# Column counts of a four-layer graph kernel: partial counts on the vector engine in place of count matmuls

## The chip, the cores and the metric

The kernel runs on one core of one Trainium2 (trn2) chip. The metric is the device time of one execution in microseconds (us). Each kernel was timed in rounds that alternate it with the kernel before on the same chip.

The engines in the profile are PE (TensorE, matmuls), PEld (its weight loads), DVE (VectorE), ACT (ScalarE), POOL (GpSimd) and SP. L552 means line 552 of that kernel's source; the lines after the edit move by 18, so L541 of the kernel before and L559 of the kernel after are both the count matmul.

## The reference, cut to what matters

Four graph layers work on `x` (2708 x 512) with one dense 2708 x 2708 adjacency matrix. Only the first layer is touched:

```python
def _L0_gnn_ref(cur, incidence_m):
    mask = incidence_m > 0
    head = mask.astype(incidence_m.dtype)
    head = head / jnp.maximum(jnp.sqrt(jnp.sum(head * head, axis=-1, keepdims=True)), EPS)
    inc = incidence_m + head
    edge_fea = inc @ cur
    edge_degree = jnp.sum(inc, axis=-1, keepdims=True)
    return edge_fea / edge_degree
...
x = _layernorm(x + _L0_gnn_ref(x, adj), axis=-1)
```

So before the product can start for some nodes, the number of nonzero entries of their rows of `adj` must be known: `inc` is `adj` plus `count ** -0.5` wherever `adj` is nonzero.

## The kernel before

The kernel holds `adj` transposed, so a destination node is a column and a count runs down the partitions. One pass over the matrix is a *sweep*; the first sweep is layer 0. It goes through four *ranges* of destination columns (256, 384, 384 and 330 wide, numbered 0 to 3), each in two halves h = 0 and 1 of the matrix, and each half has 22 row tiles of 128 rows. Ranges 1 to 3 use a seven-product scheme for 2 x 2 blocks, which needs sums of blocks such as s1 = A21 + A22, made by the vector engine just ahead of the matmuls that use them. While range r is multiplied, the counts of range r + 1 are made:

```python
def count_load(R0, n, h, i):            # GpSimd queue: one row tile of the later range
    ...
def count_mask(R0, n, h, i, t=None, on_vector=False):
    ...
    cnt[R0, h, i] = m = mask_tile()     # bf16, 128 x 384, six buffers
    ...
        nc.scalar.activation(m[:w, :n], t[:w, :n], AF.Sign)
        nc.scalar.activation(m[:w, :n], m[:w, :n], AF.Relu)

def count_tile(R0, n, h, i):            # TensorE: three matmuls of one column
    w = wt(i % KT)
    m = cnt.pop((R0, h, i))
    if i == 0:
        cnt[h] = bank("cnt", [P, 4])
    for j, q in enumerate(tiles_of(R0, n)):
        wq = wt(q)
        nc.tensor.matmul(cnt[h][:wq, j : j + 1], m[:w, q * P - R0 : q * P - R0 + wq], ones_bf[:w, 0:1],
                         start=i == 0 and j == 0, stop=i == NT - 1, skip_group_check=True)

def count_row(R0, n, h):                # clamp on VectorE, power on GpSimd
    ...
        nc.vector.tensor_scalar(r[: wt(q), 0, j : j + 1], ps[: wt(q), j : j + 1], 1.0, None, ALU.max)
    nc.gpsimd.tensor_tensor(r[:, 1, :m], r[:, 0, :m], neg_half.to_broadcast([P, m]), ALU.pow)

def spread_row(R0, n, h):               # TensorE transposes it into a row, ScalarE copies it
    ...
        nc.tensor.transpose(pr[:, q * P - R0 : q * P - R0 + w], r[:w, 1, j : j + 1].to_broadcast([w, P]), ident[:w, :w])
    nc.scalar.copy(row[R0, h][:, :n], pr[:, :n])

def prep0(r, R0, n, h, hj, k, a):       # VectorE: adj + mask * count ** -0.5
    nc.vector.scalar_tensor_tensor(t[:w, :n], a[:w, :n], 0.0, row[R0, h][:w, :n], ALU.is_gt, ALU.mult)
    nc.vector.tensor_tensor(a[:w, :n], a[:w, :n], t[:w, :n], ALU.add)
```

The schedule is a list of events `at(position, function)`; a unit is one phase (one product) of a range. For the later range's half h:

```python
for i in range(NT):                     # NT = 22
    q = pb + p + d * i / NT
    at(q - 0.7, lambda i=i, h=h: count_load(R1, n1, h, i))
    at(q - 0.35, lambda i=i, h=h: count_mask(R1, n1, h, i))
    at(q, lambda i=i, h=h: count_tile(R1, n1, h, i))
at(pb + p + d, lambda h=h: count_row(R1, n1, h))
at(pb + p + d + 0.15, lambda h=h: spread_row(R1, n1, h))
```

TensorE takes its matmuls in the program's order (in this kernel's trace it waits 2.28 us for a mask in front of the count triple at 90.07 us, with large matmuls behind it).

## Time and profile before

| | kernel before |
|---|---|
| median of its first 3 runs | 2988.14 us (2979.09 to 2988.84) |
| profiled span, clock | 2983.9 us, 0.994 |
| VectorE busy, 62 to 460 us | 340 of 398 us |
| TensorE's waits that the profile names, 62 to 460 us | 7.3 us |
| second sweep's first matmul | 439.2 us |

The table is read so: the edit can act only in the first sweep, so the start of the second sweep says what the edit was worth there. TensorE hardly waits between 62 us and that point; the lines are shown in the prediction.

```profile
286.64 2.47 POOL L555 TENSOR_TENSOR r<-r,neg_half 128x3 f32<-128x3 f32 x1 [19.75 <-DVE r L553]
```

After the last count triple TensorE has 12 large matmul records before the transposes, about 4 us. The power ends at 286.64 + 2.47 = 289.11 us, and the transposes start at 289.98: hidden, with 0.9 us to spare.

### The profile page before, as it was taken

Reading aid. Unit: us, or ns where it says so; the run is one execution under the profiler, and the core shown is the slowest. Engines: PE = TensorE matmul, PEld = TensorE weight load, DVE = VectorE, ACT = ScalarE, POOL = GpSimd, SP = SyncE. Lnnn points to the kernel's source line nnn. Section 1 sums busy time; section 2 is a strip of 40 time slices with the busy share of each in tenths; the row PEclk is TensorE's granted clock in tenths of the full one; section 3 lists DMA queues with packets and bytes.
Section 4 is the critical chain, followed back from the end, with each engine's and each line's share of the span. In section 5 each row is a group of like instructions: output and inputs, shape, how many; then the busy total and the mean of one; then the engine's idle time right before and its main releaser. Section 6 shows DMA issues by size and latency. Waiting matters only on the chain.

```text
span 2983.9 us, 37755 instructions
## 1 busy us (share of the span) xinstructions
PE 2930.5 (98%) x10982; PEld 1926.6 (65%) x10982; DVE 2191.4 (73%) x5376; ACT 596.3 (20%) x1145; POOL 692.6 (23%) x1240
## 2 busy tenths in 40 slices
PE   7999999999999999999999999999999999999998
PEld 6655666557665657766666666666666666665664
DVE  5889688556657675874686777867768877689786
ACT  4544200000144444551101000010000100100001
POOL 1423224233410101213112022020220322512112
PEclk9999999999999999999999999999999999999999
DMA  7665467586754333654676667565675666875562
GB/s 233 199 198 176 143 179 217 141 136 138 192 113 124 110 112 94 202 158 143 199 218 212 183 194 219 169 208 178 196 225 174 196 200 197 242 199 179 172 177 83
DMA packets 364119, 524.27 MB, mean 176 GB/s; under 512 B 57734, under 2 KB 312430, under 8 KB 363912
## 3 DMA queue, kind: packets, MB, share of 16 engines
q1 hardware_dynamic: 297556, 362.80, 43.4%
q0 software_dynamic: 57040, 148.22, 16.1%
q10 hardware_dynamic: 9316, 10.84, 1.2%
q8 instruction: 87, 1.43, 0.2%
q14 instruction: 120, 0.98, 0.1%
HBM read 431.26 MB, written 90.37 MB: 175 GB/s over the span
## 4 chain that ended last, share of the span: by engine, by line
PE 84%; issue 5%; DVE 4%; DMA 4%; ACT 1%; POOL 1%; SPq 1%; POOLq 0%; DVEq 0%; ACTq 0%
PE accc L1007 12%; PE accd L1007 12%; PE accu L1007 12%; PE ps_d L495 9%; PE accu L367 8%; PE accc L367 8%; PE accd L367 7%; PE acca L1007 6%; PE acca L367 4%; PE ps_n L1076 1%; PE accc L1012 1%; PE accu L1012 1%; PE accd L1012 1%; PE acca L1012 1%; SPq L127 1%
## 5 line engine op out<-in xcount | busy, mean ns | idle before, releaser
L967 DVE TENSOR_TENSOR z<-z 128x339 f32<-128x339 f32 (+1 forms) x966 | 468.8, 507 | 35.6 <-PE accu L1007 12.5
L1007 PE MATMUL accc<-z,t 128*128 128x338 f32 (+1 forms) x644 | 203.0, 447 | 0.0
L1007 PE MATMUL accc<-s,t 128*128 128x338 f32 (+1 forms) x644 | 197.9, 452 | 1.0 <-DVE s L967 1.0
L1007 PE MATMUL accd<-z,t 128*128 128x338 f32 (+1 forms) x644 | 195.2, 448 | 0.0
L1007 PE MATMUL accu<-z,t 128*128 128x338 f32 (+1 forms) x644 | 194.9, 448 | 0.0
L331 DVE TENSOR_TENSOR a<-a,a 128x384 f32<-128x384 f32 (+4 forms) x363 | 177.4, 511 | 13.9 <-PE accu L367 13.4
L1039 DVE TENSOR_TENSOR q<-q,accd 128x338 f32<-128x338 f32 (+1 forms) x112 | 56.4, 504 | 173.2 <-PE accd L1007 170.8
L1033 ACT COPY q<-accu 128x338 f32<-128x338 f32 (+1 forms) x84 | 34.3, 443 | 721.2 <-PE accu L1007 721.2
L449 POOL TENSOR_TENSOR rstd<-rstd,neg_half 128x1 f32<-128x1 f32 (+3 forms) x92 | 61.5, 668 | 495.1 <-DVE rstd L448 494.2
L967 DVE TENSOR_TENSOR s<-z 128x338 f32<-128x338 f32 (+1 forms) x322 | 154.2, 505 | 23.4 <-PE accc L1007 20.6
L1007 PEld LDWEIGHTS accc<-z,t 128*128 128x128 f32 x644 | 121.4, 189 | 61.3 <-issue 2.2
L1007 PEld LDWEIGHTS accc<-s,t 128*128 128x128 f32 x644 | 121.6, 192 | 59.8 <-issue 2.5
L1007 PEld LDWEIGHTS accu<-z,t 128*128 128x128 f32 x644 | 121.0, 190 | 59.0 <-issue 1.5
L1007 PEld LDWEIGHTS accd<-z,t 128*128 128x128 f32 x644 | 120.8, 190 | 58.3 <-issue 1.9
L757 DVE SCALAR_TENSOR_TENSOR deg<-a,deg 128x384 f32<-128x384 f32 (+5 forms) x168 | 81.5, 504 | 68.1 <-DMA a<-in_adjT 67.8
L127 POOL DMA_DIRECT2D Y<-y x102 | 55.3, 543 | 280.3 <-ACT y L1089 192.8
L822 ACT ACTIVATE e<-row,neg_s 128x384 f32<-128x384 f32 (+5 forms) x176 | 100.5, 571 | 86.5 <-DVE e L824 23.9
L824 DVE TENSOR_TENSOR e<-e,f 128x384 f32<-128x384 f32 (+5 forms) x176 | 87.3, 504 | 25.3 <-ACT f L823 24.2
L823 ACT ACTIVATE f<-row,neg_s 128x384 f32<-128x384 f32 (+5 forms) x176 | 99.9, 567 | 12.6 <-PE accc L367 6.4
L127 POOL DMA_DIRECT2D As<-a x132 | 71.2, 543 | 107.1 <-DVE a L331 48.8
L1089 ACT COPY y<-ps_n 128x512 f32<-128x512 f32 (+2 forms) x48 | 28.0, 584 | 322.3 <-issue 175.6
L495 PE MATMUL ps_d<-w,q 128*128 128x512 f32 (+2 forms) x192 | 88.1, 604 | 3.5 <-DVE q L1145 3.4
(655 smaller groups left out, 6173.5 us busy)
## 6 DMA issues: line engine op xcount, KB each, us to landing
z<-As SPq DMA_DIRECT2D x320, 169.5 KB
z<-As SPq DMA_DIRECT2D x320, 169.0 KB
a<-in_adjT SPq DMA_DIRECT2D x240, 192.0 KB
z<-in_adjT SPq DMA_DIRECT2D x240, 169.5 KB
z<-in_adjT SPq DMA_DIRECT2D x240, 169.0 KB
a<-in_adjT SPq DMA_DIRECT2D x120, 165.0 KB
cl<-in_adjT POOLq DMA_DIRECT2D x80, 192.0 KB, 4.5
a<-in_adjT SPq DMA_DIRECT2D x113, 128.0 KB
```

Source lines behind the costliest of these rows:

```text
L127: queue.dma_start(out=dst[:c], in_=src[:c])
L331: nc.vector.tensor_tensor(A[r, dst, k][:w, :n], A[r, a, k][:w, :n], A[r, b, k][:w, :n], op)
L367: nc.tensor.matmul(B[home, c][:, :n], X[STAT[p], k][:w, c * P : (c + 1) * P], A[r, MOV[p], k][:w, :n], start=bool(start and k == k0), stop ...
L449: nc.gpsimd.tensor_tensor(rstd[:w, 1:2], rstd[:w, 0:1], neg_half[:w], ALU.pow)
L495: nc.tensor.matmul(o, lhs(c), r, start=c == 0 and n == 0, stop=c == DC - 1, skip_group_check=True)
L757: nc.vector.scalar_tensor_tensor(d[:w, :n], a[:w, :n], 0.0, d[:w, :n], ALU.not_equal, ALU.add)
L822: nc.scalar.activation(e[:w, :n], row[R0, h][0][:w, :n], AF.Exp, bias=neg_s[:w, t : t + 1])
L823: nc.scalar.activation(f[:w, :n], row[R0, h][1][:w, :n], AF.Exp, bias=neg_s01[:w, t : t + 1])
L824: nc.vector.tensor_tensor(e[:w, :n], e[:w, :n], f[:w, :n], ALU.min)
L967: nc.vector.tensor_tensor(d[:, :n], Z[x + (k,)][:, :n], Z[y + (k,)][:, :n], op)
L1007: nc.tensor.matmul(B[home][:, :n], stat(v, k), a[:, :n], start=bool(start and k == 0), stop=k == nk - 1, skip_group_check=True)
L1012: nc.tensor.matmul(B[home][:, :n], groups[st, "R"][0][:w, c * P : (c + 1) * P], Z[p, 2, 0][:w, :n], start=False, stop=True, skip_group_che ...
```

## The change

Its intent: TensorE looks full, and 22 x 3 one-column matmuls per half-range are poor use of it. The masks are 0 or 1 in bf16, so 22 of them can be summed elementwise without rounding on the vector engine, and one triple of matmuls then counts the half-range.

```diff
+    def count_add(R0, n, h, i):
+
+        w = wt(i % KT)
+        m = cnt.pop((R0, h, i))
+        if i == 0:
+            cnt[h] = pool.tile([P, 384], BF, name="ca", tag="tmp", bufs=NTMP)
+            nc.vector.tensor_copy(cnt[h][:w, :n], m[:w, :n])
+        else:
+            nc.vector.tensor_tensor(cnt[h][:w, :n], cnt[h][:w, :n], m[:w, :n], ALU.add)
+
+    def count_end(R0, n, h):
+        t = cnt[h]
+        cnt[h] = bank("cnt", [P, 4])
+        for j, q in enumerate(tiles_of(R0, n)):
+            wq = wt(q)
+            nc.tensor.matmul(cnt[h][:wq, j : j + 1], t[:, q * P - R0 : q * P - R0 + wq], ones_bf[:, 0:1], start=True,
+                             stop=True)
+
...
-                    at(q, lambda i=i, h=h: count_tile(R1, n1, h, i))
+                    at(q, lambda i=i, h=h: count_add(R1, n1, h, i))
+                at(pb + p + d - 0.02, lambda h=h: count_end(R1, n1, h))
                 at(pb + p + d, lambda h=h: count_row(R1, n1, h))
                 at(pb + p + d + 0.15, lambda h=h: spread_row(R1, n1, h))
```

## The prediction

> **What bounds the kernel now.** I first read the page: busy shares, and the busy digits by slice.
>
> ```profile
> PE 2930.5 (98%) x10982; PEld 1926.6 (65%) x10982; DVE 2191.4 (73%) x5376; ACT 596.3 (20%) x1145; POOL 692.6 (23%) x1240
> PE   7999999999999999999999999999999999999998
> DVE  5889688556657675874686777867768877689786
> ```
>
> TensorE (PE) looks like the bound of the whole kernel, with VectorE (DVE) at 73%. But the change touches only the first sweep (the first 5 to 6 slices of 75 us), and there the DVE digits are 8, 8, 9. So I asked for the busy time of the first sweep's four ranges; from the accumulators' names, the ranges begin near 20, 120, 231 and 342 us. The first of these stretches starts at 62 us, where the counts for later ranges begin.
>
> ```profile
> 62.00:120.00 58.00, 55.38 (x357) 45.18 (x356) 49.85 (x138) 40.84 (x90) 28.60 (x52) 0.97 0.65 202
> 120.00:231.00 111.00, 111.00 (x482) 65.69 (x481) 99.72 (x244) 55.61 (x115) 34.36 (x61) 1.00 0.68 211
> 231.00:342.00 111.00, 111.00 (x482) 66.12 (x481) 88.52 (x209) 43.72 (x90) 32.98 (x55) 1.00 0.50 150
> 342.00:439.00 97.00, 93.45 (x348) 63.80 (x347) 83.45 (x211) 5.04 (x9) 25.23 (x46) 0.96 0.58 170
> ```
>
> The columns are stretch, length, then busy us of PE, PEld, DVE, ACT, POOL. PE is full in ranges 1 and 2, but DVE has only 11 and 22 us of idle time there. The views of waits say how near DVE is to the path (waiter <- releaser: us, times, longest):
>
> ```profile
> PE rs L590 <- DVE run L573: 3.2, 1, 3.2
> PE accd L367 <- DVE a L331: 0.3, 1, 0.3
> DVE r L553 <- PE cnt L541: 14.7, 6, 10.4
> DVE rd L620 <- PE rs L590: 6.5, 3, 4.3
> DVE ld L635 <- PE ps_n L478: 5.8, 4, 3.3
> ```
>
> I also matched each PE wait on DVE in the trace with the moment DVE released it. The matmuls on the sum "s1" (accd with T1, third phase of a range) start 0.04 us after their release at 162.6 us (range 1), about 5.8 us after at 271 (range 2), and 0.05 us after at 375 (range 3). So PE is full, and DVE is exactly at its heels twice. There are two bounds, and the change moves work from one to the other.
>
> **What the skill says.** "VectorE: DVE Perf Modes", the perf-mode tier table: tensor_tensor runs at 1x in fp32 and at 2x in bf16 in SBUF. The trace has no bf16 two-source add; for fp32 it agrees: the pitch below grows by 0.13 us for 128 more elements, 1.04 ns each. "TensorE: Matmul & The Clock Gate", Back-to-back issue gap: a matmul of 1 to 64 columns takes about 60 cycles, 25 ns at the stated 2.4 GHz, when isolated, more with a weight load. Here it is about 53 ns with its load (below). "Perfetto Trace Analysis", Identifying the Most-Contended Engine: matmul busy time isn't a good measure, since matmuls are pipelined. The trace agrees: a count matmul is recorded as 163 ns and occupies a third of that.
>
> **The change, part by part.** It removes the 22 x 3 count matmuls of each of six half-ranges: 396, replaced by 18. Their price is in the chain of waits: start, us, what.
>
> ```profile
> 126.26 3.87 PE accu L367 x12
> ...
> 137.08 1.40 PE accc L367 x4
> 138.48 0.05 PE cnt L541 x3
> ```
>
> Twelve large matmuls alone take 3.87 us, 0.3225 each, so four take 1.29. With a count triple, the group repeats every 1.40 + 0.05 = 1.45 us. A triple costs 0.16 us, and 132 triples 21 us; the six final triples give back about 1. PE also waits in front of count matmuls for masks from ACT, about 3 us between 62 and 100 us. Were PE the only bound, the time would fall by 20 to 24 us, to about 2966.
>
> It adds 132 DVE instructions: 126 bf16 adds and 6 copies, 88 of 384 columns and 44 of 330. The price is the pitch on DVE, not the recorded duration, as instructions overlap:
>
> ```profile
> 101.73 0.55 DVE L578 SCALAR_TENSOR_TENSOR s<-a,row 128x384 f32<-128x384 f32 x1
> 102.20 0.42 DVE L203 TENSOR_TENSOR T2A<-B22A,T1A 128x256 f32<-128x256 f32 x1
> 102.54 0.42 DVE L205 TENSOR_TENSOR T3A<-B22A,T3A 128x256 f32<-128x256 f32 x1
> ```
>
> 384 columns have a pitch of 0.47 us, 256 of 0.34: 0.07 fixed plus 1/0.96 ns a column. At 2x, 384 bf16 columns are an estimate of 0.07 + 0.20 = 0.27 us (recorded about 0.35), 330 are 0.24. An add set between two dependent adds costs less, about 0.15, because the dependent pair now pays 0.455 for 256 columns against 0.335 undisturbed. In all 21 x 0.27 + 11 x 0.15 + 56 x 0.27 + 44 x 0.24 = 33 us more on DVE. ACT's masks and the loads are unchanged; mask buffers now come free when DVE, not PE, has read them.
>
> **Where this lands.** The order in which the built program puts the instructions on DVE has 32 of the adds ahead of the first T3 sum, 53 ahead of range 1's last s1, 97 ahead of range 2's, all 132 ahead of range 3's. The final count also needs the last add, so PE is tied to DVE at six points. In the kernel before, DVE's lead there was small:
>
> ```profile
> 220.73 0.29 DVE L553 TENSOR_SCALAR r<-cnt 128x1 f32<-128x1 f32 x3 [1.50 <-PE cnt L541]
> 286.20 0.29 DVE L553 TENSOR_SCALAR r<-cnt 128x1 f32<-128x1 f32 x3 [0.15 <-PE cnt L541]
> 332.27 0.29 DVE L553 TENSOR_SCALAR r<-cnt 128x1 f32<-128x1 f32 x3 [1.46 <-PE cnt L541]
> ```
>
> The ledger of DVE's lateness D, adds minus the waits on PE (all in the trace) that a late DVE no longer has: at 99.5 us, 7.3 - 3.1 (its wait for the T3 matmuls) = +4. At 164, 21 more adds, 5.7, less 1.4 of waits: +8; PE had no slack, so PE is +8. At 221, 35 more, 9.4, less about 4.8: +13; PE, DVE's lead 1.5 off, is +11.5. At 286, 22 of 330 columns, 5.3, less the 4.3 of the wait of rd for rs and part of the 2.8 us before the memset at 223.85: +13, PE +13. At 332, 5.3 more, while up to 12.7 us of waits on PE can vanish, but no more than PE lets: PE, with 22 triples fewer (3.5), comes at +9.5, and D ends there. Range 3 has no adds, and DVE feeds PE without slack at 375, so the sweep ends 9 us late. The 21 us saved on PE are waited away at the ties. After the first sweep nothing is changed, and the offset stays to the end.
>
> **Rivals.** (1) PE alone is the bound: -20 to -24 us, 2966. For it: PE 111 of 111 us. Against it: the two points without slack. It needs adds of under about 0.2 us or DVE waits that vanish entirely (about 30 us of its idle time between 62 and 375 us is waiting on PE). (2) The bf16 adds run at 1x, 0.47 us: 26 us more, of which perhaps 15 to 20 stay on the path: 3010 to 3017. For it, only that the trace shows no such add. (3) The adds wait on ACT's masks and hold up what stands behind them in DVE's order, and DVE's lateness passes through POOL's layernorm powers to the next loads and masks: +5 to +15 more. ACT makes a mask each 1.0 us with six buffers of lead, so I give it little.
>
> **Number and chances.** 2988 + 9 = 2997; I shade towards rival 1, since the ledger may absorb too little: 2995. Rivals 1 and 2 are softened by the other bound, so 2977 to 3012 should hold 8 in 10. Both ends are inside 2% (60 us): within 2% 0.97, faster 0.01, slower 0.02.
>
> **What would show it.** The adds at a mean near 350 ns (550 would be rival 2); PE idle of 15 us or more in 62 to 382 us put down to DVE, at the count matmuls, s1 and s3; DVE busy over 105 of ranges 1 and 2's 111 us; range 1's s1 phase some 8 us later than before. It is wrong if PE stays full, with the start of the second sweep (439 us before) near 418, or if the time differs mainly after the first sweep.

## More of the kernel before

One path that matters later did not wait in this kernel, and so does not show among the waits. It is the round trip of the last count of a half-range, here range 3's first half, in the timeline of TensorE and then of GpSimd (columns: start us, duration us, engine, line, operation, out<-in, sizes, count):

```profile
285.93 0.23 PE L541 MATMUL cnt<-ones_bf,mask 74*128 74x1 bf16 x3
286.02 4.12 PE L367 MATMUL accu<-a,T2C 128*128 128x384 f32 x12
289.98 0.45 PE L563 MATMUL pr<-ident,r 128*128 128x128 f32 x3
```

## The result, and the profile after

The kernel after took 2996.02 us (median of 4 runs, 2993.04 to 3002.65) against 2986.40 us (median of 4, 2979.09 to 2988.84). The ratio is 1.0039, 95% interval 1.0015 to 1.0063: within 2%, and slower by a little. The profiled spans are 2983.9 us before (clock 0.994) and 2991.2 us after (0.991). The second sweep's first matmul moved from 439.25 to 448.81 us: +9.6 us.

Busy time and the digits of the two engines, after:

```profile
PE 2914.9 (97%) x10604; PEld 1918.2 (64%) x10604; DVE 2222.0 (74%) x5508; ACT 594.7 (20%) x1145; POOL 703.7 (24%) x1240
...
PE   7899999999999999999999999999999999999998
...
DVE  6999888565657675775686776867768877689786
```

378 matmuls are gone (10982 to 10604) and 132 vector instructions came (5376 to 5508), as planned. In the first four slices of 75 us, VectorE's digits go from 5, 8, 8, 9 to 6, 9, 9, 9. The same stretches of the first sweep as in the prediction (stretch, length, then busy us of PE, PEld, DVE, ACT, POOL, then the granted clock):

```profile
62.00:120.00 58.00, 47.24 (x221) 40.79 (x219) 54.26 (x165) 40.33 (x89) 25.82 (x45) 0.88 0.62 190
120.00:231.00 111.00, 102.55 (x349) 60.87 (x348) 104.51 (x272) 49.04 (x101) 37.84 (x57) 1.00 0.64 195
231.00:342.00 111.00, 103.18 (x339) 60.53 (x338) 100.00 (x260) 47.90 (x103) 41.37 (x64) 0.97 0.56 162
342.00:439.00 97.00, 93.00 (x350) 62.75 (x349) 84.58 (x213) 6.29 (x11) 21.45 (x39) 0.98 0.56 161
```

TensorE was full for 111 of 111 us in two of these stretches; now it is idle for 8 us in each of them, 11 in the first. VectorE is at 104.5 and 100.0. TensorE's waits from 62 to 460 us (waiter, line, releaser: us, times, longest):

```profile
PE pr L581 <- POOL r L573: 13.9, 5, 5.5
PE cnt L559 <- DVE ca L552: 10.8, 1, 10.8
PE accd L367 <- DVE a L331: 3.1, 4, 1.1
PE rs L608 <- DVE run L591: 3.0, 1, 3.0
```

With a small one of 0.6 us that is 31.4 us, against 7.3 before. A third of it is the wait for the sum of the adds (10.8 us, once, at the first final count):

```profile
94.62 0.24 PE L559 MATMUL cnt<-ones_bf,ca 128*128 128x1 bf16 x3 [10.76 <-DVE ca L552]
```

That wait has two parts. TensorE stands there from 83.86 us. ScalarE has the last mask of this half-range ready at 90.01 us, and VectorE, which runs without a gap from 86.10 us and has row sums ahead of it in its order, begins the last add at 94.22 us:

```profile
89.49 0.52 ACT L531 ACTIVATE mask<-mask 74x384 bf16<-74x384 bf16 x1
94.22 0.35 DVE L552 TENSOR_TENSOR ca<-ca,mask 74x384 bf16<-74x384 bf16 x1
```

So 6.2 us of the wait pass before the last mask exists, and 4.6 us after. ScalarE itself had waited 5.3 us at 80.46 us for a layernorm step of VectorE, with masks behind it (2.8 us in the kernel before, where the last mask was ready at 86.42 us and was counted at 86.61 us, without VectorE).

The largest part is a wait that the kernel before did not have: the transposes `pr` wait for the power on GpSimd. The chain of waits around the longest one (start us, us, what):

```profile
296.51 0.08 PE cnt L559 x3
...
296.61 0.30 DVE r L571 x3
...
297.05 6.39 POOL r L573
...
303.49 0.81 PE pr L581 x3
304.30 6.15 PE accu L367 x12
```

Three things are to be seen. First, the power takes 6.39 us, on 128 x 3 elements; it took 2.47 us at this place before, and 0.72 to 1.06 us at the seven other places in that kernel. Secondly, between the final count and the transposes TensorE now has 4 large matmul records in place of 12 (in its timeline, one group of 1.54 us after the count), mainly because the final triple stands 0.02 of a phase ahead of the count's end where the last one stood 2.5/22 = 0.11 ahead. So less is there to hide the round trip behind, and 5.5 us are waited. Thirdly, the 12 matmuls after it take 6.15 us. In the prediction's chain 12 of them took 3.87. The windows view of the next 4.6 us says why; the third number from the end is the granted clock:

```profile
303.40:308.00 4.60, 4.51 (x9) 2.72 (x10) 0.00 (x0) 1.76 (x4) 4.51 (x10) 0.50 0.77 221
```

The clock is at half after the gap. The Trainium skill, "TensorE: Matmul & The Clock Gate", Part 1: The HAM clock gate, says that the clock goes to 1.2 GHz after at least one idle window of about 3.4 us and back to 2.4 GHz after a busy one. This trace agrees in the lengths: its half-clock episodes last 3.4, 6.8 and 13.7 us, whole multiples of that window, and two of them go with the gaps of 10.8 and 5.5 us. It doesn't agree that a whole window has to be idle: the third episode follows a wait of 3.05 us, the kernel before has one of 3.4 us after a wait of 2.28 us (at 90.07 us), and the wait of 3.84 us from 194.12 us has none. Between 50 and 460 us they sum to 23.9 us after, and to 10.2 us before.

Why is the power slow? VectorE's timeline at its end:

```profile
302.14 0.55 DVE L597 TENSOR_TENSOR a<-a,s 128x384 f32<-128x384 f32 x1
310.36 0.56 DVE L408 TENSOR_TENSOR W<-W,U 128x384 f32<-128x384 f32 x1 [7.67 <-ACT U L401]
```

During the power VectorE runs without a gap up to 302.14 + 0.55 = 302.69 us. Then it stands still, waiting for a copy `U` of the very sums (`accu`) whose matmuls stand behind the waiting transposes. The power ends at 303.43 us, 0.74 us after VectorE stopped. The two other long powers of this kernel, 3.68 us from 119.09 and 4.58 us from 193.32, end 0.75 and 0.74 us after VectorE stops. The Trainium skill, "SBUF — State Buffer", SBUF: two separate sides, says that GpSimd shares a port pair with VectorE as "an exclusive lock, not a bandwidth split", against VectorE instructions with two SBUF inputs too, and that the loser is blocked for the whole of the other's instruction. The trace agrees in kind, but not in length: the power was kept out, at these three places, not for one instruction (0.55 us) but until the stream ended.

### The profile page after: what moved, and what is told of

It is laid out like the page before. It is cut to its first block, busy times and chain, and to the rows that moved or that the text cites. A ratio compares the mean times of both kernels' runs of the same rounds, so it can differ in the third digit from the quotient of the medians. Undisturbed runs are those within 1.5% of the kernel's fastest.

```text
span 2991.2 us, 37205 instructions
## 1 busy us (share of the span) xinstructions
PE 2914.9 (97%) x10604; PEld 1918.2 (64%) x10604; DVE 2222.0 (74%) x5508; ACT 594.7 (20%) x1145; POOL 703.7 (24%) x1240
## 4 chain that ended last, share of the span: by engine, by line
PE 85%; DVE 6%; issue 3%; DMA 2%; POOL 2%; ACT 1%; SPq 1%; POOLq 0%; DVEq 0%; ACTq 0%
PE accc L1026 12%; PE accd L1026 12%; PE accu L1026 12%; PE ps_d L495 10%; PE accu L367 7%; PE accd L367 7%; PE accc L367 7%; PE acca L1026 6%; PE acca L367 3%; PE accc L1031 1%; PE ps_n L1095 1%; PE accd L1031 1%; PE accu L1031 1%; PE acca L1031 1%; DVE s L596 1%
## 5 line engine op out<-in xcount | busy, mean ns | idle before, releaser
L331 DVE TENSOR_TENSOR a<-a,a 128x384 f32<-128x384 f32 (+4 forms) x363 | 177.9, 511 | 13.3 <-PE accu L367 12.8
L843 DVE TENSOR_TENSOR e<-e,f 128x384 f32<-128x384 f32 (+5 forms) x176 | 87.3, 504 | 25.8 <-ACT f L842 24.7
```

Source lines behind the costliest of these rows:

```text
L331: nc.vector.tensor_tensor(A[r, dst, k][:w, :n], A[r, a, k][:w, :n], A[r, b, k][:w, :n], op)
L843: nc.vector.tensor_tensor(e[:w, :n], e[:w, :n], f[:w, :n], ALU.min)
```

## The experiments

Twelve kernels ran. The theories that their expectations name:

- **A**: the 33 us of adds on VectorE, which paces TensorE at several points, ate the gain. Without them it shows nearly in full.
- **B**: the round trip of the final count (last add, count triple, clamp, power on GpSimd, transposes) ate it.
- **C**: VectorE paces TensorE at the s1 sums anyway, so only about 72 of the 132 triples are worth anything.
- **D**: there are two obstacles, and each is enough; both must go.
- **E**: a dense stream on VectorE holds GpSimd's power off, and that makes the round trip long.

### 1. The change without its adds

Wrong: the final triple counts the first tile alone. The check of the result nevertheless passed within its tolerance.

```diff
-        else:
-            nc.vector.tensor_tensor(cnt[h][:w, :n], cnt[h][:w, :n], m[:w, :n], ALU.add)
```

> The changed kernel without its 126 adds: the sum keeps the first mask alone, so the result is wrong on purpose. VectorE has 6 copies more than before and nothing else. Theory A (the added VectorE work is what ate the gain): TensorE keeps what it saved, 18 to 24 us faster than before, about 2964 us (ratio 0.992 to 0.994). Theory B (the new round trip of the final count, matmul, clamp, power on GpSimd, transpose, is what ate it): the round trip is still there, so most of the 15 us that TensorE waits for the power stays, and the gain is under 10 us (2976 or more).

Measured: 2987.12 us against 2982.62, ratio 1.0015 (0.9985 to 1.0046). The second sweep starts at 437.0 us, 2.3 earlier than before. The largest group of TensorE's waits from 62 us on:

```profile
PE pr L579 <- POOL r L571: 12.6, 4, 6.0
```

What follows: with 126 adds gone from VectorE there is still no gain. A is refuted as the whole story. The edit even takes away more than VectorE's time: without the adds the final triple no longer waits for the last mask either (6.2 us of the 10.8 us above). The wait for the power is nearly as long as with the adds (12.6 against 13.9 us); the powers took 5.9 and 3.3 us at the worst places.

### 2. The kernel before, with the adds into a tile that nobody reads

```diff
+                    at(q, lambda i=i, h=h: count_extra(R1, n1, h, i))   # copy for i = 0, else a bf16 add
                     at(q, lambda i=i, h=h: count_tile(R1, n1, h, i))
```

> The kernel before with all its count matmuls, and the same 132 adds and copies on VectorE into a tile that nobody reads; result right. Theory A: TensorE saves nothing and VectorE has the whole 33 us, so it is slower than before by 10 to 15 us, ratio 1.003 to 1.005, at least as slow as the changed kernel. Theory B: the round trip is that of the kernel before (four triples of matmuls and more between last count and transpose), so it is within 4 us of before.

Measured: 3002.11 us against 2982.62, ratio 1.0076 (1.0050 to 1.0102); the second sweep starts at 453.1 us, +13.8. TensorE's waits for the power are 6.2 us, and half clock 17.1 us. The ratio is above A's 1.003 to 1.005. So adds alone cost at least as much as the ledger of the prediction has (it puts VectorE 13 us late at 221 us), and B alone is refuted too. The adds are a real cost; taking them away is just not enough.

### 3. The transposes later in TensorE's order

```diff
-                at(pb + p + d + 0.15, lambda h=h: spread_row(R1, n1, h))
+                at(pb + p + d + 0.38, lambda h=h: spread_row(R1, n1, h))
```

> The changed kernel with one number changed: the transposes that wait for the power are put 0.23 of a phase (some 3.6 us of TensorE work) later in TensorE's list. Theory A: TensorE's waits for the power (15 us in six places) shrink to under 5 us, but the wait moves to the sums that VectorE makes; within 4 us of the changed kernel. Theory B: 8 to 14 us faster than the changed kernel, so at or a little below the kernel before.

Measured: 2988.34 us against 2982.62, ratio 1.0034 (1.0010 to 1.0057); second sweep at 444.4 us, 4.4 earlier than with the change as it is. The waits for the power fall from 13.9 to 8.4 us, the powers stay at 4.9, 4.6 and 5.9 us, and half clock is 30.7 us. The intervals of this ratio and of the change's own overlap, so in the time nothing is shown, and B's 8 to 14 us did not come. In the first sweep 4.4 of 9.6 us of lateness went, but only 2.0 of them by 344 us; the rest went in range 3, which has no counts to make, where this execution lacks the half-clock episode at 394 us.

### 4. The adds on GpSimd

```diff
-            nc.vector.tensor_tensor(cnt[h][:w, :n], cnt[h][:w, :n], m[:w, :n], ALU.add)
+            nc.gpsimd.tensor_tensor(cnt[h][:w, :n], cnt[h][:w, :n], m[:w, :n], ALU.add)
```

(and the copy of the first tile likewise)

> The changed kernel with its adds and copies on GpSimd in place of VectorE; result right. If GpSimd takes under 0.8 us an add and isn't held off, VectorE is relieved and TensorE keeps its saving: 5 to 20 us faster than before. Theory A allows that. If VectorE's dense stream holds GpSimd off (its power of 128x3 already took up to 6.4 us in the changed kernel), or the adds hold up the loads and layernorm powers behind them in GpSimd's order, it is slower than the changed kernel, by 10 us or more. I expect the second, 3010 us.

Measured: 3087.50 us, ratio 1.0367 (1.0340 to 1.0394), slower. The group of adds (durations in ns: least/median/longest):

```profile
L552 POOL TENSOR_TENSOR ca<-ca,mask x126: 804/920/25309, 61.8 to 429.6; 128x384 bf16<-128x384 bf16 x76, 128x330 bf16<-128x330 bf16 x38, 74x384 bf16<-74x384 bf16 x8, 74x330 bf16<-74x330 bf16 x4
```

Slower was expected, but 3010 us. An add that takes 0.92 us in the middle took up to 25.3 us. GpSimd is the wrong place beside a dense VectorE, and the same hold-off is seen on another operation. TensorE waited 36.9 us for these sums at the final counts.

### 5. Neither adds nor early transposes

Wrong as in 1.

```diff
-        else:
-            nc.vector.tensor_tensor(cnt[h][:w, :n], cnt[h][:w, :n], m[:w, :n], ALU.add)
...
-                at(pb + p + d + 0.15, lambda h=h: spread_row(R1, n1, h))
+                at(pb + p + d + (0.38 if h else 0.9), lambda h=h: spread_row(R1, n1, h))
```

> The changed kernel without the 126 adds (as in no_adds), and the transposes that wait for the power later in TensorE's list: by 0.75 of a phase for the first half of a range, 0.23 for the second. TensorE's waits for the power (12.6 us in no_adds) should fall under 4 us. Theory B (the round trip of the final count ate the gain): 18 to 22 us faster than before, ratio near 0.993. Theory C (VectorE, without a single add, still paces TensorE at the s1 sums of ranges 1 and 3, so TensorE's saving counts only for the 72 triples between about 164 and 342 us, 0.16 us each): 8 to 12 us faster, ratio 0.996 to 0.997, with the end of range 1's s1 phase no more than 4 us earlier than before.

Measured: 2967.07 us against 2981.28, ratio 0.9962 (0.9936 to 0.9988); second sweep at 421.5 us, 17.7 earlier. TensorE's waits for the power:

```profile
PE pr L579 <- POOL r L571: 4.0, 1, 4.0
```

Here the gain is, nearly whole, in the first sweep: -17.7 of some -20. B expected -18 to -22 and C -8 to -12, both for the time. The sweep speaks for B; the ratio, -11 us with an interval from -19 to -4, is C's, and so is its clause on range 1's s1 phase, whose end is only 1.5 us earlier. But what held TensorE there was again the power, 5.15 us from 107.73 us: the wait of 4.0 us for it and the half clock from 111.8 us took 7 us back. In the profiled execution the gain did not shrink after the sweep: the last matmuls are 19.9 us earlier than in the kernel before. Together with 1 to 3: undo one obstacle and little comes (-2.3; or +5.2 instead of +9.6), undo both and the gain is there.

### 6 and 7. VectorE relieved in another way

Both are wrong (relative error 0.107): the first sweep's row sums lose their adds, which takes 102 instructions off VectorE (the expectations say 86) while the new adds stay.

```diff
+            made.append(1)
+            if len(made) <= 8:
+                nc.vector.tensor_scalar(run[R0, h][:, :n], t[:, :n], 1.0, None, ALU.add)
+            else:
+                nc.vector.tensor_copy(run[R0, h][:, :n], t[:, :n])
-        else:
+        elif len(made) > 8:
             nc.vector.tensor_tensor(run[R0, h][:w, :n], run[R0, h][:w, :n], t[:w, :n], ALU.add)
```

The kernel before, so edited:

> The kernel before with another load taken off VectorE: the 86 adds of the row sums in the first sweep are left out (wrong on purpose), some 29 us of pitch between 62 and 382 us. Theory C: TensorE loses only what it waits for VectorE today, 5 to 10 us faster than before.

Measured: 2978.43 us against 2981.28, ratio 0.9993 (0.9973 to 1.0013). The kernel before gains next to nothing from 42 us less of busy VectorE (2191.4 to 2149.0); one of its powers took 8.6 us, and TensorE waited 5.4 us for it.

The change, so edited:

> The changed kernel with the same 86 row sum adds left out (wrong on purpose): VectorE has about as much work as in the kernel before. Theory C, and A: with room on VectorE the change pays, 10 us or more faster than before_norun. Theory B: the round trip still eats it, within 4 us of before_norun.

Measured: 2986.07 us against 2981.28, ratio 1.0015 (0.9996 to 1.0034). Second sweep at 441.3 us, +2.1. The waits for the power are 15.3 us, half clock 30.7 us.

What follows: VectorE is busy for 43 us less than with the change as it is (2222.0 to 2179.0), more than the 31 us that the change had added (2191.4 to 2222.0). That doesn't make the change pay, as long as the transposes are early. B said within 4 us of before_norun, and it is about 7 us slower; A and C expected a gain and are further off. The wait for the adds at the first final count is still 8.3 us here.

### 8. The change only in range 2, the transposes late

Range 2 makes range 3's counts, and is where VectorE had its largest idle time (22 us of 111).

```diff
-                    at(q, lambda i=i, h=h: count_add(R1, n1, h, i))
-                at(pb + p + d - 0.02, lambda h=h: count_end(R1, n1, h))
+                    at(q, lambda i=i, h=h: (count_add if r == 2 else count_tile)(R1, n1, h, i))
+                if r == 2:
+                    at(pb + p + d - 0.02, lambda h=h: count_end(R1, n1, h))
...
-                at(pb + p + d + 0.15, lambda h=h: spread_row(R1, n1, h))
+                at(pb + p + d + (0.9 if r == 2 and not h else 0.15), lambda h=h: spread_row(R1, n1, h))
```

> The change made in range 2 alone (its 44 masks are those of range 3), where VectorE was idle for 22 us; counts for ranges 1 and 2 on TensorE as before; the first half's transposes 0.75 of a phase later. TensorE saves 44 triples, 7 us; VectorE has 44 x 0.24 = 11 us more, in idle time. Theory C: 2 to 7 us faster than before, ratio 0.998 to 0.999; range 3 starts some 5 us earlier. If any add costs time wherever it stands: 2 to 5 us slower.

Measured (5 rounds): 2977.79 us against 2981.28, ratio 0.9990 (0.9972 to 1.0009). Second sweep at 432.0 us, 7.2 earlier. Of that, 1.1 us was there at 230 us, before the edit can act; the rest is near the price of its 42 triples (0.16 x 42 = 6.7 us), with a wait for row sums grown from 3.2 to 5.8 us and half clock fallen from 10.2 to 3.4 us. The power in question took 6.7 us here too, behind the large matmuls, and harmed nobody. About 5 of the 7 us were lost near 561 us, where the chain of the second sweep has a transfer of adjacency tiles of 12.75 us that ends when it ends; but the same execution is 5.8 us ahead again at 763 us and 6.5 us at the end. The ratio is inside C's range. It is worth some 3 us, and its interval includes no gain at all.

### 9. The change, relieved as in 7, and the transposes late

Wrong (relative error 0.107).

> The changed kernel with its adds, with the row sum adds left out (wrong on purpose, as in after_norun), and with the transposes later as in no_adds_late. Both obstacles are then gone with the adds in place: VectorE has room, and TensorE has other work while the power is under way. Theory D (either obstacle alone keeps most of the 21 us; both have to go): 10 to 18 us faster than before, ratio 0.994 to 0.997, waits for the power under 5 us. If the adds cost by something other than VectorE's time (mask buffers, ACT): no faster than after_norun, 1.001.

The edit is that of 7 with that of 5's last line. Measured: 2986.78 us against 2978.18, ratio 1.0024 (1.0002 to 1.0046). D, as I had put it, expected 10 to 18 us faster: it failed. The power on GpSimd and the waits for it:

```profile
185.30 14.36 POOL L573 TENSOR_TENSOR r<-r,neg_half 128x3 f32<-128x3 f32 x1 [11.62 <-DVE r L571]
```

```profile
PE pr L581 <- POOL r L573: 15.0, 3, 8.4
PE cnt L559 <- DVE ca L552: 8.8, 2, 8.3
```

A later place for the transposes doesn't help if the power grows as much: 14.4 us here, and 12.9 us at the other place. A VectorE with fewer waits of its own has a longer unbroken stream, and the power ends when the stream does. It ended 0.75 us after VectorE's last instruction in both cases. That made E out of D: the obstacle on GpSimd's side isn't the place of the transposes alone, but the power's being held off. The edit didn't remove the other obstacle either: TensorE still waits 8.3 us at the first final count, 6.1 of them before the last mask is ready at 88.98 us. So this run doesn't test D as it was meant.

### 10. The change only in range 2, the transposes early

Experiment 8 without its last line.

> As range2_late, but with the first half's transposes at the place of the changed kernel. The power near 286 us took 6.7 us in range2_late, hidden by 0.75 of a phase of matmuls. Theory D: here TensorE waits some 5 us for it and then runs at half clock for 3.4 or 6.8 us, so all of the gain is gone: 0 to 6 us slower than before, ratio 1.000 to 1.002. If the round trip doesn't matter: the same as range2_late, 0.999.

Measured (5 rounds): 2982.03 us against 2978.18, ratio 1.0012 (0.9994 to 1.0030). Second sweep at 443.0 us, +3.8, where the late one had -7.2. The power took 7.8 us, TensorE waited 5.6 us for it once, and half clock is 17.1 us against 3.4. The place of one set of transposes was all that differed in the programs, but not all of those 11 us are its price: at 284 us, before it can act, this execution is already 2.7 us behind that of experiment 8, with two half-clock episodes (at 90 and 275 us) that the other lacks. The other 8.3 us come at the round trip: the wait of 5.6 us, and the half-clock episode of 6.8 us from 295.0 us, which loses 3.4 us. The ratio is what D expected.

### 11. Range 2, and range 1's second half

```diff
+                if r == 2 or r == 1 and h:      # the other line of experiment 8 likewise
```

> As range2_late, and also the second half of range 1 (22 masks more, on VectorE between about 180 and 221 us). TensorE saves 66 triples, 11 us. Theory D: VectorE has nearly 5 us of waits on TensorE there, against 22 x 0.27 = 6 us of adds, so 2 us better than range2_late at best: 4 to 9 us faster than before, ratio 0.997 to 0.9987; not more than 2 us worse than range2_late.

Measured (5 rounds): 2975.20 us against 2978.18, ratio 0.9986 (0.9971 to 1.0000); second sweep at 430.3 us, 9.0 earlier, of which 2.6 us were there at 170 us, before the edit can act. The result is correct and the ratio as expected. It is the best correct version: its interval ends just at 1, so against the kernel before it is a gain of 3 to 4 us at most suggested; against the change as it is, whose interval starts at 1.0015, it is faster.

### 12. The change, with VectorE made to stand still for the power

The result of the power is copied by VectorE, and the transposes read the copy. VectorE's copy must wait for the power (0.78 us below), so it has no stream to hold it off with.

```diff
         nc.gpsimd.tensor_tensor(r[:, 1, :m], r[:, 0, :m], neg_half.to_broadcast([P, m]), ALU.pow)
+        nc.vector.tensor_copy(r[:, 0, :m], r[:, 1, :m])
...
-            nc.tensor.transpose(pr[...], r[:w, 1, j : j + 1].to_broadcast([w, P]),
+            nc.tensor.transpose(pr[...], r[:w, 0, j : j + 1].to_broadcast([w, P]),
```

> The changed kernel with one thing added: after each power VectorE copies its result (128x3) in place before it goes on, so VectorE stands still while GpSimd computes the power; in the built order at most two instructions of VectorE are between clamp and copy. Transposes at the changed kernel's early place. Theory E (the power is slow because VectorE's dense stream holds GpSimd off, and TensorE's wait for it and the half clock after it are most of what ate the gain): each power takes 0.7 to 1.2 us in place of up to 6.4, TensorE's waits for the power fall from 15 to under 8 us, at most one half-clock episode of the three in the sweep stays after 62 us beside the one near 87 us, and the time falls by 5 to 10 us against the changed kernel: ratio 0.9995 to 1.002 against before. Theory A (VectorE's own time is what counts): VectorE loses eight times some 0.9 us more, so 3 to 7 us slower than the changed kernel, ratio 1.005 or more.

Measured (5 rounds): 2986.01 us against 2981.76, ratio 1.0009 (0.9993 to 1.0025). GpSimd's and VectorE's timelines at the place where the power took 6.39 us:

```profile
296.68 1.07 POOL L573 TENSOR_TENSOR r<-r,neg_half 128x3 f32<-128x3 f32 x1 [10.20 <-DVE r L571]
```

```profile
297.78 0.17 DVE L574 COPY r<-r 128x3 f32<-128x3 f32 x1 [0.78 <-POOL r L573]
```

and TensorE's waits for the adds and at the transposes:

```profile
PE cnt L559 <- DVE ca L552: 10.8, 1, 10.8
PE pr L582 <- DVE r L574: 3.5, 5, 1.2
```

VectorE gives up 0.78 us and every power now takes at most 1.07 us; the waits at the transposes fall from 13.9 to 3.5 us, and the second sweep starts at 442.0 us, 6.8 earlier than with the change as it is. So E holds for powers and waits, and the ratio is where E put it; but its interval and that of the change (1.0015 to 1.0063) overlap, so in the time this is at the edge of the noise. One clause of it missed: half clock stayed at 27.3 us, 13.7 of it around the wait of 10.8 us at the first final count, which this edit leaves. What remains, +2.8 us in the sweep, I put down to the adds and their ties; that is not tested.

### The runs laid side by side

TensorE's account for the first sweep, an estimate from what the traces show: 0.16 us for each triple removed (132 less the 6 final ones in the change); plus the change of its waits (62 to 460 us) against 7.3 us; plus half of the change of half-clock time (50 to 460 us) against 10.2 us, as half is what such time loses.

| kernel | triples | waits, us | half clock, us | account, us | second sweep's start, measured |
|---|---|---|---|---|---|
| the change | -20.2 | 31.4 | 23.9 | +10.8 | +9.6 |
| 1 no adds | -20.2 | 19.0 | 20.5 | -3.3 | -2.3 |
| 2 extra adds | 0 | 16.6 | 17.1 | +12.8 | +13.8 |
| 3 late transposes | -20.2 | 22.2 | 30.7 | +5.0 | +5.2 |
| 5 no adds, late | -20.2 | 9.3 | 6.8 | -19.9 | -17.7 |
| 8 range 2, late | -6.7 | 9.3 | 3.4 | -8.1 | -7.2 |
| 10 range 2, early | -6.7 | 15.1 | 17.1 | +4.6 | +3.8 |
| 11 ranges 1 and 2 | -10.1 | 10.0 | 6.8 | -9.1 | -9.0 |
| 12 standing still | -20.2 | 22.4 | 27.3 | +3.5 | +2.8 |
| 7 no row sums | -20.2 | 24.7 | 30.7 | +7.5 | +2.1 |
| 9 the same, late | -20.2 | 25.8 | 23.9 | +5.2 | +0.3 |

In nine kernels the account closes within 2.2 us, and in the two without row sums it is 5 us too high. (Not in the table: the kernel before without row sums, account -0.9, measured -1.9; and experiment 4.) But the sum counts half-clock time that falls into idle time too, which loses nothing. With that left out, from the same traces, the two without row sums come to +1.9 and +1.2 us and close as well; the change, 3 and 12, in which 8 to 10 us of half clock are idle, then come to +6.5, +1.2 and -0.9 us, 3 to 4 us too low. So the account is good to about 4 us, and part of its agreement is two errors that cancel.

Each start of the second sweep is that of one profiled execution. At 55 to 170 us, where a program is still that of the kernel before, executions already lie between 1.0 us later and 2.6 us earlier, so differences under some 3 us say nothing. The main steps are larger, and stand at 344 us too, ahead of range 3: the change is 11.7 us late there, 1 is 1.7 early, 2 is 16.0 late, 3 is 9.7 late, 5 is 13.0 early, and 12 is 3.8 late.

## Why the prediction was right or wrong

**The number.** 2995 was predicted and 2996.02 measured, inside the range. That the number fits so well is partly luck, as the parts below show.

**The price of the triples and of an add: right.** Both are in the traces. The adds have a median of 348 ns (350 predicted), and a pitch of 0.27 us for 384 and 0.24 us for 330 columns (95.98 to 96.25 us and 293.26 to 293.50 us in the kernel after), just the estimates. Rival 2, an add at 1x, is out. That 42 triples are worth 6.7 us fits experiment 8 (-7.2, or -6.1 from 230 us on), whose waits and half clock changed a little too.

**The ledger: right at its ends, too high between.** I paired the same instructions of both traces. The first T3 sum is 4.8 us late (ledger: +4). TensorE at range 1's s1 is 5 us late at its start and 10 at its end (+8). The clamps at 221 and 286 us are 10.5 and 10.4 late (+13), TensorE at 294 us 13.6 (+13). But TensorE's large matmuls are only 5.5 us late at 222 us (+11.5) and 8.0 at 284 (+13): the clamps follow the final triple, which stands later in TensorE's order than the last one stood. The clamp at 332 us is 12.8 late (+9.5: too low), the sweep's end 9.6 (+9). Experiment 2, adds without anything saved, makes the sweep 13.8 us longer. That adds on VectorE cost TensorE time is thus shown.

**"All of it is VectorE's lateness": wrong, this step failed.** The prediction said that TensorE's waits would be put down to DVE, at the count matmuls, s1 and s3. In the stretch that it named, 62 to 382 us, TensorE waits 27.8 us. Half of that, 13.9 us (10.8 and 3.1), is put down to DVE, under the 15 that it named, and the other half, 13.9 us, to POOL. (The 3.0 and 0.6 us come after 382 us.) The prediction tied TensorE to VectorE at the final counts, and overlooked that the same edit moved the final count nearer to the transposes, so that a round trip over two other engines came into view. In its third rival GpSimd came only as the maker of the layernorm's powers. That rival, to which it gave little, is in the profile in part: the last mask of the first half-range is ready 3.6 us later than in the kernel before, and 6.2 of the 10.8 us at the first final count pass before it is there. The ledger still came out, I think, because the two causes overlap: while TensorE waits for the power, VectorE catches up on its adds. That is argued from the traces, not tested.

**"Free adds would give -20 to -24" (rival 1): wrong as put.** Experiment 1 is more than that case, as it unties the masks too, and gave -2.3 us in the sweep and nothing in the time. The gain comes only when the round trip is hidden as well (experiment 5: -17.7 in the sweep, ratio 0.9962). How much of that gain adds that are free, but still wait for their masks, would keep was not tested.

**VectorE busy over 105 of 111 us: missed.** 104.5 and 100.0. I took the lateness for a full VectorE; it stood still for up to 7.7 us at a time, waiting through `U` for TensorE, which waited for the power.

**"After the first sweep nothing is changed, and the offset stays": right within a few us.** Matched matmul by matmul, the rest of the kernel is late by 7.0 to 9.6 us, 7.3 at the end. In other kernels the offset wanders more: experiment 8 goes from 7.2 us early to 2.5 and back to 6.5, experiment 10 from 3.8 late to 3.0 early.

**What makes the power slow.** Over the 14 kernels, 23 powers took over 3 us. In 19 of them the power ended 0.74 to 0.76 us after VectorE's last instruction, before VectorE's next; in the other 4 it ended inside VectorE's stream, after 3.1 to 6.7 us. In three of these 4 (experiments 5, 8 and 11) the last 0.75 us begin at a seam of the stream: VectorE's next instruction starts 0.05 us after, 0.01 us before and 0.03 us after the end of the one ahead of it, where they otherwise overlap by about 0.08 us. That it is VectorE's stream is shown by experiment 12, which breaks the stream and otherwise only adds a copy of 128 x 3. So in the kernel after there is a ring: the transposes wait for the power, the power for VectorE to run out of work, and VectorE runs out when it needs what stands behind the transposes.

**What stays open.** When a stream holds a power off: 28 powers of 0.85 to 2.5 us also ended inside a stream, 22 of them beside only 3 or 4 instructions of VectorE, so a stream alone isn't enough. Why experiment 5 is 19.9 us ahead in its profiled execution and -11 us by the ratio, which compares four executions with eleven. Half-clock episodes later in the kernel, but for the one at its very end, sum to 7 to 24 us and differ between executions, so differences of 0.1% are at the edge of what these runs can tell.

## What to carry to other kernels

When work moves from a full engine to a nearly full one, list every tie between the two, but also every short chain over a third engine that the work was hiding: a final step that needs all the others is tied to the slowest of them, and replacing many small steps by one at the end moves the end of the chain as well, and a chain that never showed among the waits can become the largest of them. Try both obstacles together, not only each alone: here each edit by itself looked useless. In such a chain, a tiny GpSimd instruction is best given a moment in which VectorE stands still (here at most 1.07 us in place of up to 6.39), or put far ahead of its reader.

## What the Trainium skill lacked or had wrong

- "SBUF — State Buffer", SBUF: two separate sides, has the loser of the shared port pair blocked for the other's instruction. Against a dense stream of VectorE instructions of 0.25 to 0.56 us, a GpSimd power of 128 x 3, 0.88 us undisturbed, took up to 14.36 us, over 33 VectorE instructions, and in 19 of 23 long cases until VectorE stood still, ending 0.74 to 0.76 us later. No page says that the hold-off can last for a whole stream.
- "GPSIMD Engine Reference", 4.1 Engine selection, puts a two-input elementwise operation at about twice VectorE's time. Here a bf16 add of mostly 384 columns took 920 ns in the median (804 at the least) on GpSimd and 348 ns on VectorE, 2.6 times, and up to 25.3 us. All of these adds ran beside a working VectorE, so it is no clean comparison.
- No page that I found says how much idle time it takes to bring half clock. "TensorE: Matmul & The Clock Gate", Part 1: The HAM clock gate, has at least one idle window of about 3.4 us. Here half clock followed a wait of 2.28 us in the kernel before, and did not follow one of 3.84 us in the kernel after.
